# Self-loop rows as a one on the diagonal, left-overs moved inside a gathered sum, and slots, routing and scatters at other steps of a graph block on one core

## The chip, the cores and the metric

The kernel runs on one core of a Trainium2 chip. The metric is the device time of one execution in microseconds (us), as a median over several executions. The engines are PE (matrix multiply; PEld is its weight load), DVE (vector), ACT (scalar, activation), POOL (GpSimd, which here issues the indirect DMAs) and SP (which issues most plain DMAs). Each engine runs its own instructions strictly in order; between engines, semaphores hold an instruction until what it needs is there.

## What is computed

A graph block over 6,250 nodes of 256 features with 200,000 edges, then a mixture of eight experts:

```python
xn = _layernorm(x)
x = x + gnn(edge_index, xn, W, b) + mix(xn, ...)       # mix: linear attention, LN, GELU MLP, LN
x = x + ffn(_layernorm(x), gate_w, gate_b, w1, b1, w2, b2)

def gnn(A, X, W, b):                                   # GCN with self-loops
    src = concatenate([A[0], arange(N)]); dst = concatenate([A[1], arange(N)])
    dinv = rsqrt(segment_sum(1, dst))
    h = X @ W
    return relu(segment_sum(h[src] * dinv[src] * dinv[dst], dst) + b)

def ffn(h, ...):                                       # top-1 of 8 experts, capacity 977
    idx = argmax(softmax(x @ gate_w + gate_b)); pos = running count of each expert
    buf[idx, pos] = x  (dropped beyond capacity); y = expert MLP(buf); row * probability
```

The self-loop is what matters below: each node adds its own row `h[i]` once to its own sum.

## The kernel before, in words

Nodes are cut into 49 tiles of 128 (`NB`); pairs of tiles make 25 groups. The opening (up to some 266 us) normalizes x, builds a table of scaled rows `tab` (`source(t)` is its tile t) and sorts the edges into lists. The middle, from 266 us to about 1246 us, sums over edges, runs the mixer and the routing, and scatters each token's row into `xbuf`. The end runs the experts.

In the middle three Python generators are interleaved by hand, and their order is what the engines get; nothing reorders it. There are 363 places (33 x 11); at each place `dense` takes one step, then `rounds` about one, then `gather` about one and a half.

`dense` computes the sums of 32 of the 49 node tiles (`DTS`). For tile u it first counts, in 11 parts p, how many edges go from each node to each: DVE makes one-hot matrices `lo` and `hi` (line 1134), PE multiplies them into `bp` (line 1177), ACT casts `bp` into the byte matrix `A[source row, source tile, target row]` (lines 1181 and 1184). While tile u is counted, tile u-1 is summed: at parts p = 1 to 10, ACT widens one share of 4 or 5 source tiles of A to `A_r` (line 1165, function `widened`, issued one part earlier), and PE adds `A_r.T @ tab` for each of them into `ps_d` (line 1199). Before these 49 products stand two others at p = 1: an identity times the tile's own rows, which is the self-loop (line 1195), and a one-hot `ohl` times `left`, a tile of edges that found no place in the lists (line 1196). After p = 10 ACT and DVE move the sum out (lines 1121 and 1126). `ps_d` has one buffer, `bp` two, `lo` and `hi` three, `A_r` and `A` two.

`gather` computes the other 17 tiles (`GTS`). POOL gathers 128 table rows for each of 33 lists of a tile (line 1230, nine buffers, issued seven lists ahead), DVE makes their one-hots `oh` (line 1245, four ahead), and PE adds them into `ps` (line 1256). Each sum begins with the identity product (line 1253) and has, before its list e = 2, the product with the left-overs (line 1255), whose one-hot `ohg` DVE makes at e = 0 (line 1242).

`rounds` works in rounds of 14 steps. Functions are put at steps with `at(k, f, ...)`. For group c, whose sums are taken in round c+3 (k is that round's first step), `add_bias` stands at k-2, `to_slot` (lines 1390 and 1391: node number, then relu(sum) + x, into one of three `slot` buffers) at k+1, `slot_stats` at k+2, `slot_norm` at k+12, the gate at k+15. After every second group `routing` runs for the two as a generator that is walked on once per listed step: maximum and difference at k+17, exponential on ACT at k+18, then DVE blocks (from lines 1290, 1300, 1316 and 1328 on), one PE product between them (line 1311), and four scatters of rows into `xbuf` by POOL (line 1337). The same steps carry the mixer of another group: attention at steps 2 to 5 of a round (lines 1453 to 1466), `mixed` at 4, statistics at 6 and 7, roots at 8 and 9.

A buffer's next writer waits for its last readers, also for those issued later in the program: group c+2's `to_slot` stands at k+29 of group c's count and takes the buffer of group c-1, whose scatters stand at k+30.

Of the kernel before, what the change touches and what calls it, by code (L numbers as in the profile page):

```python
# [10 lines left out]
U8 = mybir.dt.uint8  # L11
FR = mybir.dt.float32r
AF = mybir.ActivationFunctionType
OP = mybir.AluOpType
# [4 lines left out]
P = 128  # L19
# [3 lines left out]
NB = 49  # L23
# [16 lines left out]
DTS = [t for t in range(NB) if t not in GTS]  # L40
# [9 lines left out]
EB = 33  # L50
# [11 lines left out]
TAILC = 22  # L62
# [13 lines left out]
def graph_block_kernel(  # L76
# [5 lines left out]
    nc = tc.nc  # L82
    V = nc.vector
# [12 lines left out]
    const = ctx.enter_context(tc.tile_pool(name="const", bufs=1))  # L96
# [46 lines left out]
    def source(t):  # L143
        o, at = table(t)
        return o[:, at, :]
# [56 lines left out]
    identr = const.tile([P, P], FR, name="ident")  # L202
    ident = identr.bitcast(F32)
    V.tensor_scalar(identr, jp, 0.0, None, op0=OP.is_equal)
    upto = const.tile([P, P], F32, name="upto")
    put_off = []

# [4 lines left out]
    Z = Later()  # L212

    def settle(n):
        for f, a, k in put_off[:n]:
            f(*a, **k)
        del put_off[:n]

    Z.tensor_scalar(upto, jp, 0.0, None, op0=OP.is_ge)
    ones = const.tile([P, P], F32, name="ones")  # L220
    V.memset(ones, 1.0)
# [709 lines left out]
    with tc.manual_schedule():  # L931
# [5 lines left out]
        f, c = 1, 0  # L937
# [174 lines left out]
    with tc.manual_schedule():  # L1112
# [39 lines left out]
        def dense():  # L1152

            mats, made, parts = {}, [], {}
            acc_ps = ohl = None
            half = NG // 4

            def share(p):
                return (p - 1) * NB // (half - 1), p * NB // (half - 1)

            def widened(u, p):

                s0, s1 = share(p)
                o = parts[p] = de.tile([P, 5, P], FR, name="A_r", tag="A_r")
                nc.scalar.copy(o[:, :s1 - s0, :], mats[u][:, s0:s1, :])  # L1165

            two = twice(0)
            made.append((0, 0, onehots(two, 0)))
            def counted():
                if made and made[0][:2] < (u, p):  # L1170
                    uu, pp, (lo, hi) = made.pop(0)
                    for i in range(2):
                        g = 4 * pp + 2 * i
                        bp = bps.tile([P, 512], F32, name="bp", tag="bp")
                        both = bp[:, :2 * NB * GN].rearrange("p (s k) -> p s k", k=2 * GN)
                        for h in range(2):
                            nc.tensor.matmul(both[:, :, h * GN:(h + 1) * GN], lo[:, 2 * i + h, :],  # L1177
                                             hi[:, 2 * i + h, :NB * GN].rearrange("p (s k) -> p s k", k=GN),
                                             start=True, stop=True)
                        if g < NL:  # L1180
                            nc.scalar.copy(mats[uu][:, :, GN * g:GN * (g + 2)], both)  # L1181
                        else:
                            at = GN * NL + 2 * (g - NL)
                            nc.scalar.copy(mats[uu][:, :, at:at + 4].rearrange("p s (g k) -> p s g k", g=2),
                                           both.rearrange("p s (g k) -> p s g k", g=2)[:, :, :, :2])

            for u in range(ND + 1):
                for p in range(half):
                    if p == 1:
                        counted()  # L1190
                    if u >= 1 and p >= 1:

                        if p == 1:
                            acc_ps = dps.tile([P, 2 * D], F32, name="ps_d", tag="ps_d")
                            nc.tensor.matmul(acc_ps, identr, source(DTS[u - 1]), start=True, stop=False)
                            nc.tensor.matmul(acc_ps, ohl, left, start=False, stop=False)
                        A, (s0, s1) = parts.pop(p), share(p)
                        for hi in range(s0, s1):
                            nc.tensor.matmul(acc_ps, A[:, hi - s0, :], source(hi), start=False, stop=(hi == NB - 1))  # L1199
                    if u < ND:  # L1200
                        if p == 0:
                            mats[u] = de.tile([P, NB, P], U8, name="A", tag="A")
                        if p == half - 2 and u + 1 < ND:
                            two2 = twice(u + 1)
                        if p < half - 1:
                            made.append((u, p + 1, onehots(two, p + 1)))
                        elif u + 1 < ND:
                            two = two2
                            made.append((u + 1, 0, onehots(two, 0)))
                    if u >= 1 and 0 < p < half - 1:  # L1210
                        widened(u - 1, p + 1)
                    if u < ND and p == half - 3:
                        ohl = de.tile([P, P], FR, name="ohl", tag="ohl", bufs=1)
                        V.tensor_scalar(ohl, rowb, dsub[:, DTS[u]:DTS[u] + 1], None, op0=OP.is_equal)
                    if u >= 1 and p == half - 1:
                        put_sum(DTS[u - 1], acc_ps)
                        put_rest(DTS[u - 1], acc_ps)
                    if p != 1:
                        counted()
                    if u >= 1 and p == 0:  # L1220
                        widened(u - 1, 1)
                    yield

        def gather():
            tiles, ohs = {}, {}
            ps = rest = None
            for j in range(NGT + LAG):
                if j < NGT:
                    gt = tiles[j] = ga.tile([P, 2 * D], FR, name="gt", tag="gt")
                    nc.gpsimd.indirect_dma_start(  # L1230
                        out=gt, out_offset=None, in_=g_dram,
                        in_offset=bass.IndirectOffsetOnAxis(ap=idxs[j // P][:, j % P:j % P + 1], axis=0))
                    if j % P == P - 1:
                        sources(j // P + 2)
                if rest is not None:
                    put_rest(*rest)
                    rest = None
                i = j - LAG
                m = i + AHEAD
                if i >= 0 and i % EB == 0:  # L1240
                    ohg = ga.tile([P, P], FR, name="ohg", tag="ohg", bufs=1)
                    V.tensor_scalar(ohg, rowb, dsub[:, GTS[i // EB]:GTS[i // EB] + 1], None, op0=OP.is_equal)
                if 0 <= m < NGT and m % 2 == 0:
                    oh = ga.tile([P, 2, P], FR, name="oh", tag="oh", bufs=3)
                    V.tensor_tensor(oh, rowb.unsqueeze(1).to_broadcast([P, 2, P]),  # L1245
                                    rel[:, m:m + 2].unsqueeze(2).to_broadcast([P, 2, P]), op=OP.is_equal)
                    ohs[m], ohs[m + 1] = oh[:, 0, :], oh[:, 1, :]
                if i >= 0:
                    k, e = divmod(i, EB)
                    t = GTS[k]  # L1250
                    if e == 0:
                        ps = gps.tile([P, 2 * D], F32, name="ps", tag="ps")
                        nc.tensor.matmul(ps, identr, source(t), start=True, stop=False)
                    if e == 2:
                        nc.tensor.matmul(ps, ohg, left, start=False, stop=False)
                    nc.tensor.matmul(ps, ohs.pop(i), tiles.pop(i), start=False, stop=(e == EB - 1))  # L1256
                    if e == EB - 1:
                        put_sum(t, ps)
                        rest = t, ps
                yield  # L1260
            put_rest(*rest)
# [82 lines left out]
        def rounds():  # L1344
# [194 lines left out]
            def at(k, f, *args):  # L1539
                plan.setdefault(k, []).append((f, args))  # L1540
# [40 lines left out]
            for c, r in takes.items():  # L1581
                k = S_ * r - (2 if c == TAILC - 1 else 0)
                needs[k - 2] = c
                at(k - 2, add_bias, c)
                at(k + 1, to_slot, c)
                at(k + 2, slot_stats, c, 4)
                at(k + 12, slot_norm, c, 4)
                at(k + 13, slot_turn, c)
                at(k + 14, slot_turned, c)
# [11 lines left out]
                if c % 2:  # L1601
                    def begin(c=c):
                        b = batches[c - 1]
                        b[1] = routing([c - 1, c], b[0], slots)
                        walk(b[1])

                    at(k + 17, begin)
                    soon = (18, 19, 19, 21, 21, 22, 23, 23, 24, 24)
                    sooner = (18, 22, 23, 24, 25, 26, 27, 27, 28, 28)
                    for d in soon if c == TAILC - 1 else sooner if c == TAILC - 3 else (18, 24, 25, 27, 28, 29, 30, 30, 31, 32):  # L1610
                        at(k + d, lambda c=c: walk(batches[c - 1][1]))
            for r in range(NGR):
                at(S_ * r + (6 if r == NGR - 1 else 8), start_roots)
# [347 lines left out]
```

## Time and profile before

| | |
|---|---|
| median of 9 runs | 1600.42 us (1594.3 to 1604.46) |
| profiled execution, own time | 1599.83 us |
| its span | 1598.0 us |
| mean granted PE clock | 0.963 |
| opening, 0 to 270 us: PE busy, DVE busy | 231.58, 202.69 us |
| middle, 300 to 1300 us: PE, DVE, ACT, POOL busy | 895.02, 706.35, 635.88, 606.22 us |
| end, 1400 to 1598 us: PE busy | 178.86 of 198 us |
| `to_slot`'s first instruction (L1390) x22: DVE idle before it | 57.6 us, 10 times |
| scatters into `xbuf` (L1337) x46 | mean 1057 ns |
| product with the left-overs, dense (L1196) x32 | median 397 ns |

"Busy" is the time in which an engine works on an instruction. Matmuls overlap, so the start of one to the start of the next is what one adds, not its duration. Idle time is named by what released the engine; "issue" means that the profile shows no releaser, "remote" that it came from outside the engines.

### The profile page before, as it was taken

Reading aid. Unit: us, or ns where it says so; the run is one execution under the profiler, and the core shown is the slowest. Engines: PE = TensorE matmul, PEld = TensorE weight load, DVE = VectorE, ACT = ScalarE, POOL = GpSimd, SP = SyncE. Lnnn points to the kernel's source line nnn. Section 1 sums busy time; section 2 is a strip of 40 time slices with the busy share of each in tenths; the row PEclk is TensorE's granted clock in tenths of the full one; section 3 lists DMA queues with packets and bytes.
Section 4 is the critical chain, followed back from the end, with each engine's and each line's share of the span. In section 5 each row is a group of like instructions: output and inputs, shape, how many; then the busy total and the mean of one; then the engine's idle time right before and its main releaser. Section 6 shows DMA issues by size and latency. Waiting matters only on the chain. (4 is left out here: it accounts for less than half of the span.)

```text
span 1598.0 us, 22383 instructions
## 1 busy us (share of the span) xinstructions
PE 1432.1 (90%) x7002; PEld 1038.7 (65%) x7002; DVE 1010.9 (63%) x3435; ACT 903.6 (57%) x2051; POOL 733.8 (46%) x725
## 2 busy tenths in 40 slices
PE   5998996989998989898988988989888899999996
PEld 2665664666666766666666666666666567766864
DVE  6786786667776777777776767777776323322332
ACT  2775654657675757676666676766665342433321
POOL 0103525666665666666666665766672210111110
PEclk9999997999999999999999999999999899999998
DMA  8438766776777667777676767677665353234030
GB/s 255 144 117 283 222 205 179 179 176 171 183 183 189 171 180 191 187 184 205 172 197 168 196 173 195 158 198 185 176 162 164 127 169 120 96 135 140 30 118 13
DMA packets 173459, 267.52 MB, mean 167 GB/s; under 512 B 26409, under 2 KB 73984, under 8 KB 173318
## 3 DMA queue, kind: packets, MB, share of 16 engines
q0 software_dynamic: 89168, 166.39, 40.5%
q1 hardware_dynamic: 83268, 98.39, 19.1%
q10 hardware_dynamic: 882, 1.05, 0.4%
q8 instruction: 65, 1.06, 0.3%
q14 instruction: 76, 0.62, 0.1%
HBM read 208.05 MB, written 60.39 MB: 168 GB/s over the span
## 5 line engine op out<-in xcount | busy, mean ns | idle before, releaser
L1230 POOL DMA_INDIRECT gt<-g_dram,idxc x561 | 581.8, 1037 | 323.0 <-PE ps L1256 130.6
L1199 PE MATMUL ps_d<-tab,A_r 128*128 128x512 f32 x1568 | 436.5, 409 | 18.3 <-issue 9.6
L1181 ACT CAST A<-bp 128x294 uint8<-128x294 f32 x640 | 241.8, 431 | 265.1 <-PE bp L1177 121.8
L1199 PEld LDWEIGHTS ps_d<-tab,A_r 128*128 128x128 f32 x1568 | 298.4, 194 | 104.5 <-ACT A_r L1165 20.7
L1177 PE MATMUL bp<-hi,lo 128*128 128x147 bf16 x1408 | 196.4, 268 | 79.9 <-ACT A L1181 31.5
L1165 ACT CAST A_r<-A 128x640 fp32r<-128x640 uint8 (+1 forms) x320 | 230.7, 723 | 14.2 <-PE ps_d L1199 6.3
L1177 PEld LDWEIGHTS <-lo 128*128 128x128 bf16 x1408 | 109.8, 106 | 188.2 <-issue 147.0
L1256 PE MATMUL ps<-gt,oh 128*128 128x512 f32 x561 | 224.7, 459 | 0.0
L1134 DVE TENSOR_TENSOR lo<-rowb,two 128x512 bf16<-128x512 bf16 x352 | 148.0, 421 | 58.1 <-PE bp L1177 19.1
L1838 POOL DMA_INDIRECT out<-rep,who x43 | 42.6, 991 | 280.7 <-DVE rep L1835 226.6
L1804 PE MATMUL hpf<-xet,w1e 128*128 128x128 f32 (+3 forms) x576 | 158.0, 432 | 8.4 <-ACTq L1916 3.5
L1245 DVE TENSOR_TENSOR oh<-rowb,rel 128x256 fp32r<-128x256 bf16 x281 | 116.9, 416 | 75.5 <-PE ps L1256 49.2
L1134 DVE TENSOR_TENSOR hi<-hib,two 128x592 bf16<-128x592 bf16 x352 | 162.1, 461 | 0.0
L1814 PE MATMUL ypf<-w2e,hm 128*128 128x256 f32 (+1 forms) x688 | 151.4, 379 | 0.0
L1814 PEld LDWEIGHTS ypf<-w2e,hm 128*128 128x128 f32 (+1 forms) x688 | 128.8, 188 | 21.6 <-issue 3.1
L1804 PEld LDWEIGHTS hpf<-xet,w1e 128*128 128x128 f32 x576 | 92.6, 199 | 65.9 <-issue 54.7
L1806 ACT ACTIVATE hm<-hpf,fb_s 128x128 f32<-128x128 f32 (+3 forms) x144 | 72.4, 514 | 87.1 <-PE hpf L1804 84.5
L1256 PEld LDWEIGHTS ps<-gt,oh 128*128 128x128 f32 x561 | 99.6, 200 | 4.8 <-issue 0.3
L1816 DVE TENSOR_TENSOR y<-ypf,fb_s 128x256 f32<-128x256 f32 (+1 forms) x43 | 18.2, 423 | 133.1 <-PE ypf L1814 133.1
L892 PE MATMUL mm<-wqkv_s,xnt 128*128 128x512 f32 (+1 forms) x196 | 93.4, 599 | 0.3 <-DVE tab L481 0.3
L1817 ACT ACTIVATE y<-y,xe 128x256 f32<-128x256 f32 (+1 forms) x43 | 21.9, 508 | 125.8 <-DVE y L1816 125.8
L1337 POOL DMA_INDIRECT xbuf<-slot,put x46 | 48.6, 1057 | 59.6 <-ACT A L1379 26.7
(376 smaller groups left out, 2007.7 us busy)
## 6 DMA issues: line engine op xcount, KB each, us to landing
g_dram<-tab SPq DMA_DIRECT2D x24, 512.0 KB
xbuf<-zeros SPq DMA_DIRECT2D x26, 384.0 KB
gt<-g_dram,idxc POOLq DMA_INDIRECT x561
w1e<-in_fw SPq DMA_DIRECT2D x8, 1024.0 KB
w2e<-in_fw SPq DMA_DIRECT2D x8, 1024.0 KB
xe<-xbuf SPq DMA_DIRECT2D x7, 1028.0 KB
xt<-in_x SPq DMA_DIRECT2D x28, 256.0 KB
xe<-xbuf SPq DMA_DIRECT2D x9, 771.0 KB
```

The source lines that it names most:

```text
L892: nc.tensor.matmul(kp[:r, :], xnt[:, c, i * r:i * r + r], wqkv_s[:, c, D:3 * D], start=(c == 0), stop=(c == 1))
L1134: V.tensor_tensor(one.rearrange("p g (w t) -> p g w t", t=2), row.rearrange("p (w t) -> p w t", t=2).unsqueeze(1).to_broadcast([P, 4, w // ...
L1165: nc.scalar.copy(o[:, :s1 - s0, :], mats[u][:, s0:s1, :])
L1177: nc.tensor.matmul(both[:, :, h * GN:(h + 1) * GN], lo[:, 2 * i + h, :], hi[:, 2 * i + h, :NB * GN].rearrange("p (s k) -> p s k", k=GN), s ...
L1181: nc.scalar.copy(mats[uu][:, :, GN * g:GN * (g + 2)], both)
L1199: nc.tensor.matmul(acc_ps, A[:, hi - s0, :], source(hi), start=False, stop=(hi == NB - 1))
L1230: nc.gpsimd.indirect_dma_start(out=gt, out_offset=None, in_=g_dram, in_offset=bass.IndirectOffsetOnAxis(ap=idxs[j // P][:, j % P:j % P + 1 ...
L1245: V.tensor_tensor(oh, rowb.unsqueeze(1).to_broadcast([P, 2, P]), rel[:, m:m + 2].unsqueeze(2).to_broadcast([P, 2, P]), op=OP.is_equal)
L1256: nc.tensor.matmul(ps, ohs.pop(i), tiles.pop(i), start=False, stop=(e == EB - 1))
L1804: nc.tensor.matmul(hp[:, :nn], w1e[:, c, f * P:(f + 1) * P], xet[:, c, at:at + nn], start=(c == 0), stop=(c == 1))
L1806: nc.scalar.activation(hm[:, f, :nn], hp[:, :nn], AF.Relu, bias=fb1_s[:, e * 8 + f:e * 8 + f + 1])
L1814: nc.tensor.matmul(yp[:r, :], hm[:, f, (i - i0) * P:(i - i0) * P + r], w2e[:, f, :], start=(f == 0), stop=(f == FF - 1))
```

## The change

Four edits. (1) In `dense` the identity product is dropped. Instead DVE adds an identity of bytes, `ident8`, to the tile's own square of the byte matrix A, at part p = 2; `ident8` is made once in the opening, among the operations that are put off there. `share` now depends on the tile: the ten shares are the same, but taken in a rotated order, so that the one with the own square comes at p = 6. The product with the left-overs opens the sum. (2) In `gather` the product with the left-overs moves from list 2 to list 16. (3) `to_slot` and `slot_stats` move from k+1 and k+2 to k+3 and k+4. (4) The walks of `routing` move from k+24 to k+32 to k+20 to k+28 for all pairs but the last (which keeps its own), and the special list of the pair that ends with group 19 goes.

```diff
+    ident8 = const.tile([P, P], U8, name="ident8")
...
+    Z.tensor_copy(ident8, ident)
...
-            def share(p):
-                return (p - 1) * NB // (half - 1), p * NB // (half - 1)
+            def share(u, p):
+                n = half - 1
+                own = next(c for c in range(n) if DTS[u] < (c + 1) * NB // n)
+                c = (own + p - 1 - n // 2) % n
+                return c * NB // n, (c + 1) * NB // n
 
             def widened(u, p):
-                s0, s1 = share(p)
+                s0, s1 = share(u, p)
...
                         if p == 1:
                             acc_ps = dps.tile([P, 2 * D], F32, name="ps_d", tag="ps_d")
-                            nc.tensor.matmul(acc_ps, identr, source(DTS[u - 1]), start=True, stop=False)
-                            nc.tensor.matmul(acc_ps, ohl, left, start=False, stop=False)
-                        A, (s0, s1) = parts.pop(p), share(p)
+                            nc.tensor.matmul(acc_ps, ohl, left, start=True, stop=False)
+                        A, (s0, s1) = parts.pop(p), share(u - 1, p)
                         for hi in range(s0, s1):
-                            nc.tensor.matmul(acc_ps, A[:, hi - s0, :], source(hi), start=False, stop=(hi == NB - 1))
+                            nc.tensor.matmul(acc_ps, A[:, hi - s0, :], source(hi), start=False, stop=(p == half - 1 and hi == s1 - 1))
+                    if u >= 1 and p == 2:
+                        own = mats[u - 1][:, DTS[u - 1], :]
+                        V.tensor_tensor(own, own, ident8, op=OP.add)
...
-                    if e == 2:
+                    if e == EB // 2:
                         nc.tensor.matmul(ps, ohg, left, start=False, stop=False)
...
-                at(k + 1, to_slot, c)
-                at(k + 2, slot_stats, c, 4)
+                at(k + 3, to_slot, c)
+                at(k + 4, slot_stats, c, 4)
...
                     soon = (18, 19, 19, 21, 21, 22, 23, 23, 24, 24)
-                    sooner = (18, 22, 23, 24, 25, 26, 27, 27, 28, 28)
-                    for d in soon if c == TAILC - 1 else sooner if c == TAILC - 3 else (18, 24, 25, 27, 28, 29, 30, 30, 31, 32):
+                    for d in soon if c == TAILC - 1 else (18, 20, 21, 23, 25, 25, 26, 26, 27, 28):
```

## The prediction

> **What bounds the kernel now.** I read the page's busy shares first, then the waits, then the timeline at the places the change touches.
>
> ```profile
> PE 1432.1 (90%) x7002; PEld 1038.7 (65%) x7002; DVE 1010.9 (63%) x3435; ACT 903.6 (57%) x2051; POOL 733.8 (46%) x725
> ...
> PE   5998996989998989898988988989888899999996
> ...
> DVE  6786786667776777777776767777776323322332
> ```
>
> PE is the bound: over 8 tenths in nearly every slice. From 440 to 1246 us its timeline has gaps over 0.8 us that sum to some 68 us. A microsecond saved counts where PE runs without a gap, or where it ends one; it is lost where PE then waits for another engine. The end of the span follows the middle, so what the middle gains the whole gains.
>
> The waits of DVE between 266 and 1246 us, as total, times and longest:
>
> ```profile
> DVE slot L1390 <- DMA xbuf<-slot,put: 42.0, 7, 6.7
> ...
> DVE slot L1390 <- issue: 15.6, 3, 6.0
> ```
>
> Ten times `to_slot` holds DVE for 4 to 7 us until the scatters have freed its slot: 57.6 us. How much reaches PE is read at one place, first DVE's timeline, then PE's (start, duration, idle before):
>
> ```profile
> 476.12 0.16 DVE L1333 SCALAR_TENSOR_TENSOR put<-kept,pos 128x4 int32<-128x4 f32 x1
> 481.84 0.17 DVE L1390 CAST slot<-pid 128x2 int32<-128x2 f32 x1 [5.56 <-issue]
> ...
> 482.92 0.28 DVE L1242 TENSOR_SCALAR ohg<-rowb,dsub 128x128 fp32r<-128x128 bf16 x1
> ```
>
> ```profile
> 480.59 0.65 PE L1453 MATMUL mm<-kvb,q 128*128 128x132 f32 x4
> 483.25 0.50 PE L1255 MATMUL ps<-left,ohg 128*128 128x512 f32 x1 [2.00 <-DVE ohg L1242]
> 483.58 0.78 PE L1256 MATMUL ps<-gt,oh 128*128 128x512 f32 x2
> 484.16 2.34 PE L1199 MATMUL ps_d<-tab,A_r 128*128 128x512 f32 x5
> ```
>
> `ohg` stands behind the stalled `to_slot`, so PE loses 2.0 us; then five products take 2.34 us where they usually take 1.33. The windows say why (PE busy, PEld, DVE, ACT, POOL, then granted clock):
>
> ```profile
> 484.00:486.00 2.00, 2.00 (x6) 1.39 (x5) 1.93 (x9) 0.00 (x0) 1.44 (x2) 0.50 1.01 325
> 486.00:488.00 2.00, 2.00 (x10) 1.15 (x9) 1.83 (x7) 0.21 (x1) 1.58 (x2) 0.67 1.00 336
> ```
>
> The clock is halved for some 3.4 us after the gap, which costs another 1.7 us.
>
> **The change part by part.** *The scatters before the slot.* The walks end four steps earlier and `to_slot` stands two later: the first scatter of group c-1 goes from k+30 to k+26, the `to_slot` that needs its buffer from k+29 to k+31. One of 363 places lasts 980/363 = 2.70 us, so five steps are 13.5 us of room, against the 5.7 us from `put` to `to_slot` above. The wait should go. What it is worth on PE I sum from the gaps that end within 6 us after a stall, or wait for `ohg`: 2.01 (at 481 us), 1.28 (722), 1.16 (877), 1.24 (1114), 0.81 (1170), 1.48 and 1.58 (1185 and 1188) = 9.6 us. The half clock after 484 us adds 1.7; that from 1187 to 1194 us (0.63 and 0.51 granted in two windows of 4 us) another 3.4. After the other stalls PE runs on from the one-hots made ahead. I take 9.6 + 1.7 = **11.3 us**, lowest 4.1 (only the three gaps before L1255, which the move to list 16 ends by itself), highest 14.7.
>
> The Trainium skill ("TensorE: Matmul & The Clock Gate", section on HAM oscillation) wants no idle gap over about 3.4 us. This trace is stricter: a 2.00 us gap was followed by half clock. By the page's rule no clock would be won here and the estimate would be 9.6.
>
> *The identity product.* 32 fall away:
>
> ```profile
> L1195 PE MATMUL ps_d<-tab,ident 128*128 128x512 f32 x32 | 17.2, 536 | 0.0
> ```
>
> 536 ns is duration; what one adds is its start to the start of the next, and that depends on ACT. PE, then ACT, around one of them:
>
> ```profile
> 1030.99 0.55 PE L1177 MATMUL bp<-hi,lo 128*128 128x147 bf16 x4 [0.76 <-ACT A L1184]
> 1031.33 0.48 PE L1195 MATMUL ps_d<-tab,ident 128*128 128x512 f32 x1
> 1031.65 0.39 PE L1196 MATMUL ps_d<-left,ohl 128*128 128x512 f32 x1
> 1031.88 1.18 PE L1199 MATMUL ps_d<-tab,A_r 128*128 128x512 f32 x4
> ```
>
> ```profile
> 1030.62 0.55 ACT L1184 CAST A<-bp 128x196 uint8<-128x196 f32 x2
> 1031.20 0.62 ACT L1165 CAST A_r<-A 128x512 fp32r<-128x512 uint8 x1
> ```
>
> Identity to left-overs is 0.32 us, left-overs to the first share 0.23. The first share was ready at 1031.82, only 0.06 before PE came. So here the identity covered ACT's cast: without it PE waits as long. Going through all 32, the cast ended 0.31 us or more before its use in 16 of them and less than 0.18 before in 16. In the free half PE wins 0.24 us (the left-overs now open the sum and keep the 0.32): 16 x 0.24 = **3.8 us**. In the tight half I take nothing: the rotation mostly puts a share of five first, cast in 734 ns instead of 619, so the 0.1 us of slack is used up; the share of four comes later and gives its product back there. Bounds: 0 if ACT holds everywhere, 32 x 0.32 = 10.2 if nowhere. The page's spacing for 512 columns (same title, section on the back-to-back gap) is 216 ns, which would make 6.9 over 32; it does not see the wait for ACT.
>
> *The added bytes.* 32 DVE additions of 128x128 bytes are in no row. Near ones: 128x256 with two float inputs takes 422 to 432 ns, 128x8 takes 168; in between by width, 0.29 us, or 9.3 us in all. The addition stands before p = 2's one-hots and waits for ACT's last cast of that matrix, which ended 0.16 to 3.5 us before the old L1195 at p = 1, so DVE comes after it. The share that waits for it is widened three places (8 us) later. The cover is DVE's idle time, some 27% of the middle. I charge **1 us**; 9.3 if all shows; nothing at best. `ident8` is one more such operation in the opening, where DVE is idle a quarter of the time: 0, at most 0.3.
>
> *Steps moved on DVE.* `to_slot` (0.68 us from start to start at 481.84) and `slot_stats` (1.08) now meet attention (1.31 at steps 3 and 5) and `mixed` (0.60); two routing blocks (1.29 and 1.45, from 463.48 and 466.73 us) meet statistics at steps 6 and 7 (1.08 each). With one-hots (0.71 a place and 0.24 for `oh`) steps 3 to 7 of every second round hold 4.74 + 2.62 + 0.68 + 3.24 + 0.60 + 2.74 = 14.6 us against 13.5: DVE ends 1.1 us late, 1.9 with one addition and one L1126. What hides this is the lead: `lo` and `hi` are used two places (5.4 us) after they are issued, `oh` four lists. 0; without cover 10 x 1.9 = 19. The next routing block follows its exponential on ACT by two steps (5.4 us) instead of six, enough for ACT unless it stalls.
>
> *Queues.* POOL passes the four scatters of each pair ahead of about six gathers; same number, 1.06 us each, and `put` still stands one step before them. Seven lists of lead (four places and a half, 12 us) cover two scatters in a row. PE's routing product moves from step 13, among the transposes, to step 9, where no other function asks for its PSUM pool. On SP only one order changes: the last group's x and q are loaded before group 20's store, waiting for its `to_slot`; they are needed nine steps later. The x and sum buffers are freed two steps later; x is asked for two steps after that.
>
> **Sum.** -11.3 - 3.8 + 1 = -14.1 us from the profiled 1599.83 (span 1598.0 and 1.8 around it): 1585.7. That execution lies 0.6 below the median, so 1586.
>
> **The rivals.** *The wait moves on.* ACT takes PE's place at p = 1 in all tiles, and only the gaps before L1255 go. For it: half of the casts arrive just in time, and ACT has waits of up to 6.5 us released by "remote" with PE gaps behind them (5.6 at 568 us, 5.2 at 1045). Against: nothing makes those longer. 1600.4 - 4.1 + 1 = 1597. 13%.
>
> *DVE takes the path, slower.* In steps 3 to 7 of ten rounds DVE's lateness shows on PE, 19 us, and the other additions too, 27 x 0.29 = 7.8: 1600.4 - 15.1 + 27 = 1612. It decides once DVE at step 7 lags by more than the two places of lead. For it: DVE is the next busiest engine. Against: stalls of 5.7 us in the same rounds left PE no gap in half the cases. 8%.
>
> *POOL waits for `put` before the earlier scatters and the gathers behind it come late.* It would replace the old stall with one of PE on `gt`: ten times 1.2 us (the wait before the scatter at 1029.87) on top of 1597 is 1609. POOL is idle over a third of the middle and L1256 shows no idle time now, so 3%.
>
> **How the numbers follow.** My forecast has 76%: 1586, by its own bounds 1575 (all gains at their highest) to 1595. To leave out no more than 2 in 10 the range takes in the second case: 1575 to 1599. About 0.3% (4.8 us) can be told from no change: faster 0.77, same 0.13, slower 0.10.
>
> **What would show it.** L1390 with no idle before it, L1255 no longer waiting for `ohg`. L1199's wait for `A_r` should grow by 3 to 5 us, at p = 1. The new byte addition should take 0.25 to 0.32 us with no wait of note. If DVE is the trouble, L1177 and L1256 would wait for `lo`, `hi` or `oh` at steps 5 to 9. I am wrong if PE's gaps after the old stalls stay with another releaser, or if the half-clock windows come as often as before.

## The result, and the profile after

The changed kernel took 1619.6 us as a median of 20 runs (1610.85 to 1629.18), the kernel before 1596.3 us beside it (62 runs, 1587.59 to 1612.21): a ratio of 1.0145, interval [1.0127, 1.0163]. The forecast was 1586 us. Two runs made later gave 1.0152 [1.0106, 1.0199] and 1.013 [1.01, 1.0161]. The profiled execution of the changed kernel took 1628.24 us, its span 1626.4.

Busy time by engine, and the slices of PE and DVE, from the page of the changed kernel:

```profile
PE 1438.8 (88%) x6970; PEld 1040.6 (64%) x6970; DVE 1019.1 (63%) x3468; ACT 904.1 (56%) x2051; POOL 731.9 (45%) x725
...
PE   5998996989998989888997889988988899999996
...
DVE  6786786667785777776777676867785322422331
```

PE has 32 products less and yet 6.7 us more of busy time, at a mean granted clock of 0.952 instead of 0.963, and its share is 88% instead of 90%. The groups that the forecast spoke of (busy, mean ns of one, then idle before it and what ended that):

```profile
L1204 PE MATMUL ps_d<-tab,A_r 128*128 128x512 f32 x1568 | 443.2, 414 | 32.3 <-ACT A_r L1171 20.8 <-issue 10.4
...
L1345 POOL DMA_INDIRECT xbuf<-slot,put x46 | 57.3, 1247 | 90.4 <-ACT A L1387 23.4 <-ACT hm L1813 17.0 <-ACT slot L1387 16.6
...
L1207 DVE TENSOR_TENSOR A<-A,ident 128x128 uint8<-128x128 uint8 x32 | 9.1, 284 | 0.0
L1263 PE MATMUL ps<-left,ohg 128*128 128x512 f32 x17 | 7.6, 446 | 0.0
...
L1398 DVE CAST slot<-pid 128x2 int32<-128x2 f32 x22 | 3.9, 178 | 0.3 <-issue 0.3
```

The stall that the change is about is gone: 0.3 us of idle time before the slot's first instruction instead of 57.6. The product with the left-overs waits for nothing, and the byte addition takes 0.28 us and waits for nothing. So what the change was to do, it does. But PE waits 20.8 us for `A_r` where it waited 8.4, and POOL waits before its scatters. From the waits, the releaser that grew most (total, times, longest):

```profile
ACT A L1187 <- remote: 87.1, 27, 9.2
```

```profile
ACT A L1181 <- remote: 52.8, 20, 6.5
```

The first is the changed kernel, the second the kernel before. "remote" means that the profile names no local work that came last; that it came from outside the engines is not shown, and group 2 below finds PE behind such a wait. Both kinds of wait are followed up below. The loss has no one place: from the first dense sum to the last, the middle grew from 979.1 to 1002.1 us. At the same place of the program the changed kernel is some 2 us behind when the kernel before is at 586 us, 5 at 661, 12 at 817 and 19 at 934, and from there on it stays some 20 us behind.

POOL and the `put` it waits for, from the timeline of the changed kernel (POOL's rows and the one of `put`: start, duration, idle before):

```profile
463.67 0.94 POOL L1238 DMA_INDIRECT gt<-g_dram,idxc  x1 [0.30 <-issue]
465.99 1.10 POOL L1238 DMA_INDIRECT gt<-g_dram,idxc  x1 [1.39 <-DVE hi L1136]
470.26 0.16 DVE L1341 SCALAR_TENSOR_TENSOR put<-kept,pos 128x4 int32<-128x4 f32 x1
471.22 1.16 POOL L1345 DMA_INDIRECT xbuf<-slot,put  x1 [4.13 <-ACT slot L1387]
472.69 1.32 POOL L1345 DMA_INDIRECT xbuf<-slot,put  x1 [0.30 <-issue]
474.31 1.23 POOL L1238 DMA_INDIRECT gt<-g_dram,idxc  x1 [0.31 <-issue]
```

In the kernel before, the first scatter of the same pair:

```profile
477.62 1.04 POOL L1337 DMA_INDIRECT xbuf<-slot,put  x1 [0.30 <-issue]
```

In the changed kernel POOL has finished its gathers at 467.1 us and stands before the first scatter for 4.13 us, until 0.8 us after DVE has made `put`. The releaser named is not the cause: ACT's norm at that time is that of the next group's slot, and in all ten pairs the held scatter starts 0.79 to 0.81 us after the end of `put`, whatever ACT does then. No gather starts between 465.99 and 474.31. The ten pairs of groups up to 1250 us hold POOL for 37.9 us like this, 1.5 to 5.5 us each; in the kernel before the ten waits came to 5.4 us.

### The profile page after: what moved, and what is told of

Same layout as the page of the kernel before. It is cut to its first block, busy times and chain, and to the rows that moved or that the text cites. A ratio compares the mean times of both kernels' runs of the same rounds, so it can differ in the third digit from the quotient of the medians.

```text
span 1626.4 us, 22380 instructions
## 1 busy us (share of the span) xinstructions
PE 1438.8 (88%) x6970; PEld 1040.6 (64%) x6970; DVE 1019.1 (63%) x3468; ACT 904.1 (56%) x2051; POOL 731.9 (45%) x725
## 5 line engine op out<-in xcount | busy, mean ns | idle before, releaser
L1238 POOL DMA_INDIRECT gt<-g_dram,idxc x561 | 572.4, 1020 | 312.5 <-PE ps L1264 119.5
L1204 PE MATMUL ps_d<-tab,A_r 128*128 128x512 f32 x1568 | 443.2, 414 | 32.3 <-ACT A_r L1171 20.8
L1264 PE MATMUL ps<-gt,oh 128*128 128x512 f32 x561 | 228.3, 465 | 2.7 <-DMA gt<-g_dram,idxc 2.6
L1811 PE MATMUL hpf<-xet,w1e 128*128 128x128 f32 (+3 forms) x576 | 162.2, 440 | 10.6 <-PEq L1923 6.7
L1345 POOL DMA_INDIRECT xbuf<-slot,put x46 | 57.3, 1247 | 90.4 <-ACT A L1387 23.4
```

The lines of the kernel that those rows point to most:

```text
L1238: nc.gpsimd.indirect_dma_start(out=gt, out_offset=None, in_=g_dram, in_offset=bass.IndirectOffsetOnAxis(ap=idxs[j // P][:, j % P:j % P + 1 ...
L1811: nc.tensor.matmul(hp[:, :nn], w1e[:, c, f * P:(f + 1) * P], xet[:, c, at:at + nn], start=(c == 0), stop=(c == 1))
```

## The experiments

Eighteen runs, each timed in five rounds beside the kernel before on the same chip. They are in five groups, each on another chip, and the chips were of two kinds, which became part of the finding: in two of the groups before took 1597 to 1599 us, as on record ("slow chips" here), in the three others 1503.5 to 1505 us ("fast chips"). No chip was used twice, so whether the kind belongs to the chip or to its condition at that time is not shown. Ratios are always against before on the same chip.

### 1. Each part alone

The own row's edit alone (the diff's parts in `dense`); the place of the left-overs alone (`e == EB // 2`); the slot and the routing alone; and all but the own row.

> Before with the own row as a one in the counts' diagonal alone (rotated shares, 32 byte additions, no identity product). Theory S (the earlier scatters hold POOL until put, and the gathers behind them come late) expects 1588 to 1597 us: a small gain of 0 to 8 us, with DVE's stall at the slot as long as before (some 58 us in all). Theory O (the added byte stands between two casts of ACT, and the fixed share order makes PE wait for A_r) expects most of the loss here: 1610 to 1620 us, with PE's waits for A_r about doubled (8 to 20 us).

> Before with the left-overs of a gathered sum at list 16 instead of list 2, and nothing else. Both theories expect little: 1590 to 1597 us, the three gaps before the left-over product (2.0, 1.2 and one under 1 us) gone. If 1605 or more, neither theory holds and the place in the sum matters by itself.

> Before with the routing walked sooner and the slot filled two places later, nothing else. Theory S expects the whole loss here: 1612 to 1625 us, POOL waiting 3 to 5 us before the first scatter of each of ten pairs, the DVE stall of 58 us gone. Theory O expects the gain that was forecast: 1582 to 1590 us. Theory D (DVE late at steps 3 to 7) also expects 1612 or so, but with the loss in waits of PE for lo, hi and oh, and POOL's waits costing nothing.

> The changed kernel without the own row's edit: the routing sooner, the slot later, the left-overs at list 16. Theory S expects 1610 to 1625 us (the loss stays); theory O expects 1580 to 1590 us. If it lies halfway (1600 to 1608), both edits share the loss.

On a fast chip (before 1503.5 us): own row 1.0050 [1.0032, 1.0067], left-overs 0.9987 [0.9973, 1.0], slot and routing 0.998 [0.9969, 0.9992], all but the own row 0.9959 [0.9944, 0.9974]. Here the schedule was no loss, against theory S, and the forecast's gain did not come either. ACT had no wait for "remote" in any of these traces. The own row's span is 13.9 us longer than that of the left-overs alone. 4.2 of them come in the tail, which here is all that follows the last dense sum (see group 5), and 8.0 at one place in the middle: the slot's stall fell on `ohg` at list 2, which left PE 5.17 us idle from 454.6 us on and the clock at 0.50 from 460 to 464. Where a stall of before hits says little about the edit itself, so it is tried again below without the stall.

### 2. The whole again, and the own row taken apart

`own_mid` is before with the own row and the left-overs; `order_only` is the changed kernel with this back:

```diff
+                            nc.tensor.matmul(acc_ps, identr, source(DTS[u - 1]), start=True, stop=False)
+                            nc.tensor.matmul(acc_ps, ohl, left, start=False, stop=False)
...
-                        V.tensor_tensor(own, own, ident8, op=OP.add)
```

> The changed kernel once more, beside the parts that were run alone. Theory O (the own row's edit loses, the schedule and the place of the left-overs win) expects the sum of the parts: on a chip where before takes 1504 us 0.9959 + 0.0050 = 1.001 (1502 to 1508 us). Theory C (the loss depends on the chip: the record's 1.0145 came from executions with ACT's casts waiting for 'remote', which the runs of the parts don't show at all) expects 0.995 to 1.002 where ACT shows no such wait, and 1.010 to 1.018 where it shows 50 to 90 us of it. If it is 1.010 or more without such waits, the parts interact and neither holds.

> The kernel before once more, for its profile on the same chip. Theory C expects, where it takes some 1504 us, no wait of ACT for 'remote', ACT's casts (L1181) waiting some 180 us for PE's bp, and the granted clock at 0.98 instead of 0.963. DVE's stall at the slot should still be there, 50 to 60 us.

> Before with the own row's edit and the left-overs at list 16. In the run with the own row alone one gap of 5.17 us stood before the left-over product, with half clock behind it, some 8 us in one place. If that is the edit's whole loss (the first one-hot caught behind the slot's stall), this one is at 0.995 to 0.999 of before; if the added byte or the share order costs by itself, it is at 1.003 to 1.006 as the own row alone.

> The changed kernel with the identity product back and the byte addition out, so that of the own row's edit only the new order of the shares is left. If the addition is what loses, this is as fast as the changed kernel without the edit (0.996 of before, 1493 to 1500 us). If the order loses (a share of five first, waited for at p = 1), it is at 1.001 to 1.006 and PE's waits for A_r stay. If the identity product's going away wins by itself, it is 3 to 8 us slower than the changed kernel.

This group was on a slow chip (before 1597.2 us): changed 1.0152 [1.0106, 1.0199], before itself 0.9989 [0.9958, 1.002], own row and left-overs 1.0037 [1.001, 1.0063], changed without the addition 1.0116 [1.0072, 1.0159]. Without the schedule most of the loss is gone; with the schedule and without the addition most of it stays. The waits for "remote" were back, 39.3 us for before and 77.9 us for the changed kernel, but also 79.7 us in `own_mid`, so their sum alone does not tell a loss.

What "remote" stands for is seen in the longest of them, from the timeline of the changed kernel's first profile:

```profile
885.81 0.52 PE L1183 MATMUL bp<-hi,lo 128*128 128x147 bf16 x4
...
886.42 1.32 PE L1204 MATMUL ps_d<-tab,A_r 128*128 128x512 f32 x5
...
887.95 0.48 PE L1264 MATMUL ps<-gt,oh 128*128 128x512 f32 x1
...
894.00 0.41 ACT L1187 CAST A<-bp 128x294 uint8<-128x294 f32 x1 [9.25 <-remote]
896.80 0.41 ACT L1187 CAST A<-bp 128x294 uint8<-128x294 f32 x1 [2.39 <-remote]
...
897.88 0.80 PE L1204 MATMUL ps_d<-tab,A_r 128*128 128x512 f32 x1 [9.45 <-ACT A_r L1171]
```

By the profile, whose ends of products are modelled, PE's four `bp` products are over by 886.33 us, but ACT, idle all the while, starts on them at 894.00 and 896.80. In the trace's semaphore events PE's increments of those microseconds come one by one at 889.76, 891.86, 893.98 and 896.78 us, and then two within 0.15 us. ACT's share `A_r` comes after them, so PE stands for 9.45 us. I call such a case a late completion: ACT's cast starts more than 0.9 us after its products' modelled ends and after ACT's own work before it. A profile has 49 to 65 in 704 casts on slow chips, and none on fast ones. Whether the news of the end is late there or the product itself ended later than modelled, the profile can't tell.

### 3. The scatters' place

```diff
-(18, 20, 21, 23, 25, 25, 26, 26, 27, 28)
+(18, 20, 21, 23, 25, 25, 27, 28, 29, 30)
```

> The changed kernel again, to stand beside the other three of this call. Theory C (the loss is one of chips where completions of PE reach the other engines late) expects 1.010 to 1.018 where before takes some 1597 us and ACT waits for 'remote', and 0.997 to 1.003 where before takes some 1504 us and there is no such wait.

> The changed kernel without the own row's edit, the second time. It was 0.9959 on the chip where before takes 1504 us. On that chip all theories expect 0.994 to 0.998 again. On the other kind theory S (POOL held for put, gathers late behind it) expects 1.007 to 1.014, since the schedule is still in it; theory O (the own row alone loses) expects 0.994 to 1.000.

> The changed kernel with the four scatters at 27, 28, 29, 30 instead of 26, 26, 27, 28: still ahead of the later slot, but two places behind put instead of one, and one to a place. Theory S expects POOL's waits of 3 to 5 us before the first scatter of a pair to fall under 1.5 us, DVE's stall at the slot to stay away, and on the slow kind of chip a ratio of 0.998 to 1.005 instead of 1.015; on the fast kind 0.994 to 1.002. If POOL's hold is not the cause, the ratio stays within 0.003 of the changed kernel's.

> The same scatters at 27 to 30, without the own row's edit. Theory S expects the best of the four: 0.988 to 0.996 on either kind of chip. If the own row's edit costs nothing, it equals the one with it.

A slow chip again (before 1598.5 us): changed 1.013 [1.01, 1.0161], without the own row 1.015 [1.0114, 1.0185], scatters later 1.0055 [1.0028, 1.0083], scatters later without the own row 1.0046 [1.0015, 1.0076]. So the own row is not the loss here, and moving four POOL issues by one or two steps takes 58% of it away with the own row and 69% without. POOL's ten holds went from 35.8 us (no own row) to 14.0, longest 4.12 (that one ended 3.4 us after `put`, so `put` is not its cause); the expectation of under 1.5 us each was missed, and the ratio did not get below 1.

For the middle (places 60 to 339 of the 363, ten pairs of rounds) I split PE's time into gaps over 0.2 us, the time lost to the half clock (half the length of its windows), and the rest:

| | gaps | half clock | rest |
|---|---|---|---|
| slow chips: before, two profiles | 75.8, 70.8 | 23.9, 30.7 | 691.7, 686.2 |
| slow: changed, three profiles | 88.3, 81.1, 79.7 | 35.8, 34.1, 34.1 | 682.7, 686.3, 685.8 |
| slow: scatters later, no own row | 73.1 | 25.6 | 693.1 |
| fast: left-overs alone (2nd) | 28.5 | 3.4 | 686.9 |
| fast: changed without own row | 25.2 | 0.0 | 687.5 |

The rest lies between 683 and 693 us everywhere, and two profiles of before differ by 5.5 in it. The two kinds of chip differ by gaps and by the half clock that follows gaps, and so do the two kernels on the slow kind.

### 4. The opposite dose, and the routing apart from its scatters

All four have the left-overs at list 16 and no own row. `slot_only` moves the slot and leaves the routing where it was; the two others have the slot later, the routing's DVE blocks sooner, and these scatters:

```diff
+ (18, 20, 21, 23, 25, 25, 30, 30, 31, 32)    # scat_old_place
+ (18, 20, 21, 23, 25, 25, 25, 25, 26, 27)    # scat_sooner
```

> The left-overs at list 16 alone, the second time, as the base of the other three of this call. 0.9987 where before took 1504 us. Where before takes some 1597 us: 0.996 to 1.001 by theory S (the place of the left-overs only ends the gaps before them); 1.003 to 1.005 if the half per cent that was left in the run with the later scatters comes from the left-overs' place.

> The left-overs at list 16 and the slot filled two places later, the routing and its scatters where they were. Theory S (the scatters' place sets the loss) expects DVE's stall at the slot cut to 0 to 25 us, POOL's waits before the first scatters as before (0.3 us) and 0.994 to 1.001. If the later slot crowds DVE at steps 3 and 4 and that is what is left of the loss, 1.003 to 1.006.

> The slot later and the routing's DVE blocks sooner, as in the changed kernel without the own row, but the scatters back at 30, 30, 31, 32. Theory S expects no hold on POOL (0.3 us before a first scatter) and 0.995 to 1.001. If the sooner routing blocks on DVE cost by themselves (they were at 1.0046 with the scatters at 27 to 30), it stays at 1.003 to 1.006.

> The opposite dose: the changed kernel without the own row, with the scatters one place sooner still, at 25, 25, 26, 27, in the place of put itself. Theory S expects POOL held for 5 to 8 us before the first scatter of a pair and 1.018 to 1.030 where before takes some 1597 us; where before takes 1504 us, 1.000 to 1.010. If the hold costs nothing, it equals 1.013 to 1.015 (0.996 on the fast kind).

A fast chip (before 1504.9 us):

| slot | routing's DVE blocks | scatters | us | ratio | POOL's ten holds, us |
|---|---|---|---|---|---|
| old | old | 30-32 | 1503.37 | 0.9987 [0.9973, 1.0002] | 11.0 |
| later | old | 30-32 | 1481.88 | 0.9855 [0.9836, 0.9874] | 11.2 |
| later | sooner | 30-32 | 1489.67 | 0.9907 [0.9886, 0.9927] | 3.0 |
| later | sooner | 26-28 (from group 1) | 1497.19 | 0.9959 [0.9944, 0.9974] | 36.9 |
| later | sooner | 25-27 | 1513.88 | 1.0057 [1.0037, 1.0078] | 61.3 |

This takes the change apart. The slot two places later is worth 21.5 us by itself: it leaves 10.8 us of the stall, though the scatters stand where they were. The sooner DVE blocks give 7.8 us back (in that run the special list of the pair that ends with group 19 is gone too), the sooner scatters another 0.0052 of 1504, 7.8 us (a comparison of ratios, since that run was on another fast chip), and one step more another 15. Two expectations missed: the later slot alone was to be at 0.994 to 1.001 and gained far more, and against it the sooner blocks cost what neither theory S nor the forecast had allowed for. The one for the opposite dose held, with holds of 4.7 to 7.2 us.

Why the blocks cost is seen in two windows of the run with the later slot alone: five places around steps 13 to 17 (in the count of the groups whose routing runs, 28 steps a pair), then the five around steps 21 to 25, into which the routing moves (window and its length, then busy PE, PEld, DVE, ACT, POOL, then granted clock, DMA share and GB/s):

```profile
615.03:630.88 15.85, 15.85 (x90) 12.28 (x89) 10.61 (x31) 10.82 (x25) 11.64 (x12) 1.00 0.79 206
635.15:646.97 11.82, 11.42 (x60) 8.23 (x60) 11.14 (x45) 9.30 (x21) 8.69 (x10) 1.00 0.83 213
```

And the same two stretches of places with the routing sooner and the scatters at 30:

```profile
619.28:635.11 15.83, 15.83 (x89) 12.28 (x89) 10.63 (x31) 10.81 (x25) 12.29 (x12) 1.00 0.78 193
639.38:653.78 14.40, 12.13 (x65) 8.68 (x64) 13.48 (x57) 9.31 (x21) 10.80 (x11) 1.00 0.82 221
```

In the first stretch DVE works 10.6 of 15.9 us and PE all of it. In the second DVE works 11.1 of 11.8 us: there DVE is the bound. Twelve more DVE instructions (45 to 57) add 2.34 us of DVE work, and the stretch grows by 2.58. This pair is among those that grow most. Over the ten, these five places grow by 1.2 us a pair on average, and 0.5 us a pair is left once the time is taken off that the other places win without the blocks. On PE it shows as waits: in the ten pairs those of `A_r` grow from 3.2 to 6.9 us, and those of routing's own product for DVE's `fore` from 2.4 to 4.8.

And why the scatters cost, PE's and DVE's waits in the run with the scatters one step sooner still, and then in the run with the later slot alone:

```profile
PE ps L1256 <- DMA gt<-g_dram,idxc: 15.6, 17, 3.4
```

```profile
DVE slot L1390 <- DMA xbuf<-slot,put: 10.8, 6, 6.3
...
PE ps L1256 <- DMA gt<-g_dram,idxc: 1.8, 2, 1.5
```

In the three runs with the DVE blocks sooner, PE's wait for gathered rows goes with POOL's holds: none with 3.0 us of holds, 4.8 with 36.9, 15.6 with 61.3. It is no rule beyond them. The later slot alone has 1.8 us with 11.2 us of holds, and in its second run, with the same holds, this:

```profile
PE ps L1256 <- DMA gt<-g_dram,idxc: 5.4, 5, 2.1
```

On slow chips the three profiles of the changed kernel have 30.5 to 37.9 us of holds and only 1.4 to 3.6 us of this wait, the one without the own row 35.8 and 0.5. The scatters' place costs there too (group 3), but by which way it reaches PE is not shown.

### 5. The one part undone

`walk_undone` is the changed kernel with its last edit taken back; `slot_only_2` is the run of group 4 again.

```diff
+                    sooner = (18, 22, 23, 24, 25, 26, 27, 27, 28, 28)
-                    for d in soon if c == TAILC - 1 else (18, 20, 21, 23, 25, 25, 26, 26, 27, 28):
+                    for d in soon if c == TAILC - 1 else sooner if c == TAILC - 3 else (18, 24, 25, 27, 28, 29, 30, 30, 31, 32):
```

> The later slot and the left-overs at list 16, routing and scatters where they were, once more. Theory S with the later slot as the gain expects 0.984 to 0.988 where before takes 1504 us, as in the first run, and, where before takes some 1597 us, 0.982 to 0.994: no POOL hold to pay for, and fewer gaps and less half clock than before. If the slow kind of chip eats the gain, 0.997 to 1.003.

> The changed kernel with one part undone: the routing's steps and scatters back where they were, the own row's byte, the left-overs at list 16 and the later slot kept. If the sooner routing and scatters are the whole loss, 0.984 to 0.996 on either kind of chip, and within 0.005 of the run beside it. If the own row's edit loses as it did alone (1.0050, with a stall of DVE that is gone here), 0.989 to 0.993 on the fast kind; if it costs nothing, the two are equal.

A fast chip (before 1505.0 us): 0.9869 [0.9852, 0.9885] and 0.9897 [0.9879, 0.9915], that is 1483.95 and 1489.04 us, both as expected. The changed kernel with one edit undone is faster than before by 1.0%, and the best version leaves out the own row too. That edit costs 5 us even where the stall is gone, and not in the middle, which takes 869.5 us with it and 869.9 without (866.0 in the first run of the same). The tail takes 356.3 against 346.6 us. PE's waits with the own row's edit name a part of it:

```profile
PE hpf L1812 <- PEq L1924: 6.8, 2, 3.4
```

PE's own sequencer stops twice for 3.4 us at the experts' branches, and from the last dense sum to PE's last product the half clock costs 10.6 us instead of 3.7. The run beside it has no such stop; the first run of that kernel had one of 3.0 us and a tail of 351.9. Over all profiles the pattern is plain: the seven with the own row and the one with its share order alone have two stops each (6.6 to 6.9 us together); of the twelve others ten have one of 3.0 to 3.5 us, one has two and one has none. So the own row comes with one more stop of some 3.4 us, wherever the slot stands. What places the stops was not tried; the edit changes the number of instructions in the queues ahead of them.

## Why the prediction was wrong, by its own steps

*"The wait should go": right, but half the size.* It went (57.6 to 0.3 us). The forecast priced it at 11.3 us, from the gaps within 6 us of a stall and the half clock after two of them. The later slot by itself gave 21.5 us on a fast chip, where the stall was as long (57.8 us); on a slow one, the kind that the price was read from, it was not run alone. The PE gaps in the middle fell by half (28.5 to 14.2 us), and places further behind the stall became shorter too: over the ten pairs the three places at the stall took 9.0 us less, and three that come seven places later 11.5. What was added up was only what stood right beside a stall.

*"Steps moved on DVE ... 0": the first step that failed.* The sum was made for steps 3 to 7 of a round and against 2.70 us a place, the mean of the middle; the two blocks that go to step 25 (step 11 of the next round) are not in it. But in the profile of before the 28 places of a pair take 2.0 to 3.7 us on average, and the blocks go to steps 20 to 25, which take 2.0 to 2.8. On average, in the place around step 21 DVE was already at work for 2.15 of 2.29 us, and for 2.14 of 2.39 in the next. The rival "DVE takes the path" had the mechanism, but put it at steps 3 to 7 (17 to 21 of the pair's count), where little was lost; the cost came at steps 21 to 25, and the whole of the sooner blocks was 7.8 us on a fast chip.

*"Queues ... `put` still stands one step before them": the second.* The distance in steps did stay; in time it did not. At step 30 of before POOL stood only 0.3 us before most first scatters: the places before it are long ones that PE fills, POOL's gathers wait there for PE's products (130.6 us of idle time before L1230 in all), and `put` is made meanwhile. At steps 25 and 26 DVE is the engine behind, and POOL stands 1.5 to 5.5 us before the scatter. This was the rival given 3% and priced at ten times a wait of 1.2 us that the old place showed. The hold at the new place is three times as long: 37.9 us in ten pairs. But the rival had PE wait for gathered rows, and on slow chips that wait stayed under 4 us. On slow chips moving the scatters back by one or two steps was worth 1.0% (1.015 to 1.0046), on a fast one by four 0.5%.

*The chip: not in the forecast.* On fast chips the whole change without the own row is a small gain, 0.9959. On slow chips there are late completions as well, and the changed kernel has more gaps and half clock than before. That the late completions use up the lead and the schedule's holds then turn into gaps is a reading of the table of gaps and not shown; no run took late completions away on a slow chip. The changed kernel as a whole was not run on a fast chip, nor the left-overs or the later slot alone on a slow one, so it stays open where on slow chips the last 0.46% of the run with later scatters sits, and whether the later slot keeps its gain there.

*The own row: 3.8 us forecast against 1 us.* The addition took 0.284 us where 0.29 was estimated, and it is hidden. The products' 3.8 us did not come: on a fast chip the middle is no shorter with the edit. "L1199's wait for `A_r` should grow by 3 to 5 us" did not hold on a fast chip (11.5 us with the left-overs alone, 10.2 with the own row alone); on the slow one the growth by 12.4 us is mostly the one wait of 9.45 us behind a late completion, and the two other profiles of the changed kernel have 10.0 and 8.8 us where before has 8.4 and 3.1. The loss of 5 us with its one more stop in the tail was no term of the sum.

*The left-overs: as forecast.* 0.9987 twice; the gaps before that product are gone.

## What to carry to other kernels

Sum a moved block against the place that it moves to, not against the mean place: which engine is the bound changes within a round, and a step that is free in one half is paid in full in the other. When an instruction that waits is moved in an in-order queue, compare the two engines' progress at the new place, since a distance counted in steps is no distance in time. And of two edits against one stall, run each alone: here the later slot did the work, and the second edit gave most of it back.

## What the runs showed of the hardware

The same kernel took 1503.5 to 1505 us on some chips and 1597 to 1599 on others, 6% apart, with the granted clock at 0.98 and at 0.96. With the difference go the late completions, and the gaps and the half clock behind them: up to 8.6 us each, and 107 to 122 us summed over a profile, where fast chips show nothing over 0.04 us. On slow chips they go with DMA traffic: over the ten profiles, with under 100 GB/s in the 2 us around a product's end, 1 of 767 handovers was over 1.5 us late; between 170 and 250 GB/s 246 of 3335 were (7%). But fast chips move more (197 to 206 against 177 to 184 GB/s in places 60 to 339) and show none, so traffic alone is not the cause, which stays open. Their places are partly the program's own: over the 704 casts, the lateness in the two profiles of before on slow chips has a correlation of 0.46, in pairs of the three of the changed kernel 0.59 to 0.64.
